# A graph layer on one core: the rank-five row term as four row-tiled passes instead of four full ones

## The chip, the cores and the metric

The kernel runs on one core of one Trainium2 chip. The metric is the device time of the launch in microseconds, as the median of several runs. A profile is one further execution, recorded instruction by instruction. The engines are called PE (TensorE, with its weight loads listed apart as PEld), DVE (VectorE), ACT (ScalarE), POOL (GpSimd) and SP (SyncE, which issues all DMAs here).

## The reference, cut to what matters

64 batch items, each with 256 tokens of 768 features and a 256 x 256 matrix `adj` of zeros and ones. With `h` the normalized, rectified input:

```python
h = jnp.maximum(_layernorm(x, axis=-1), 0.0)
ctx = jnp.matmul(adj, hs @ Wadj.T + badj) / deg_c[..., None]
ctx = ctx + jnp.matmul(radj, hs @ Wrev.T + brev) / rdeg_c[..., None]
ctx = ctx + hs @ Wself.T + bself
agg = jnp.einsum('bij,bijr->bir', adj, E[rels])
rel = agg @ Wr.T + br * deg[..., None]
...
rel = rel + ragg @ Wrr.T + brr * rdeg[..., None]
return ctx + rel
```

`deg` and `rdeg` are the row and column sums of `adj`; `rels` is `adj` itself. So the relation term of a token depends on its two degrees alone, and together with the biases it is, per token, a row of five numbers (two flags "degree over 0", a one, two degrees) times a 5 x 768 matrix. This small product is what the change is about.

## The kernel before, in words

**The large products.** The three products of `h` with the weights are made for both 128-token halves of an item by a scheme of 15 block products in place of 18 (`PRODUCTS`, line 24). Each operand is split into parts in the type fp32r. A block product (`product`, line 629) is 12 matmuls of 128x128 weights and 384 columns: eight in one part and four in the other (`first` and `second`, with the order of the two depending on the place in the chain), with a scaling of the sum in PSUM by ACT between them (line 657). DVE or ACT then read the sum into one or two blocks `c` (lines 668, 677, 679). The products are done in two sweeps over all items (`SWEEPS`, line 54): eight in the first, and in the second 9, 7, 6, 15, 12, 4 and 1, in this order. Products 9, 6, 12 and 1 share a chain `x`, which stays in one pair of PSUM banks; 7 has a pair called `v`, 15 one called `u`, and 4 one called `t`. Items 1 to 62 are "regular". Items 0 and 63 use plain fp32 matmuls instead (`whole`, line 754).

**Between the sweeps** the blocks lie in DRAM. In the second sweep `step2` (line 933) does the seven products of an item and the aggregations (`aggregate`, line 909): four groups of eight fp32r matmuls with `adj` as weights, each evicted by DVE at line 928 with the division by the degree.

**The row term before.** `front2` (line 838) writes the five numbers of each token into a 128x128 tile `cols`: for each half of the tokens, two copies, 32 columns apart. A transpose on PE (line 886) turns it over, and ACT copies 64 rows of the result into the tile `half0` and the other 64 into `half1` (line 892); the other 64 rows of each tile are zeros, written once at the start (line 1075). `rows_prepare` (line 789) makes the matching right side: the 5 x 768 matrix stands four times in 128 partitions, 32 apart, once as its high part and once as what is left, alternating. Then `add_rows` in `product` (line 645) adds `half.T @ rows` to the sum of product 7 (first half of the tokens) and of product 15 (second half), just before the second block is read from it, since only that one is to contain the row term. Each addition is two matmuls of 384 columns with a contraction over 128 partitions. Items 0 and 63 do the same into a fresh pair of banks (lines 939 to 954).

**The order of the work.** All operations are first recorded with an engine, a duration, a rank (a due time) and the buffers they use. `Plan.schedule` (line 303) then builds the order in which they are issued, by a simulation: each engine takes the ready operation of lowest rank for which buffers are free. The ranks are shifted by a table of numbers for each kind of operation, `OFFSETS` (line 91). Names in it end in `@` for item 0, `@1` for item 1, `$` for item 63, `$1` for item 62. PSUM is handed out as four pairs of banks (`"Q": 4` in `SLOTS`). Once issued, each engine runs its own operations strictly in order and waits for others by semaphores.

Of the kernel before, what the change touches and what calls it, by code (L numbers as in the profile page):

```python
# [10 lines left out]
F32 = mybir.dt.float32  # L11
# [6 lines left out]
P = 128  # L18
# [47 lines left out]
        (9, "x", 0, ((1, 0, 0),)),  # L66
        (7, "v", 0, ((1, 0, 2), (1, 0, 1))),
        (6, "x", 1, ((1, 0, 1),)),
# [23 lines left out]
    "a0+a1+b0+b1": 8.69, "a0+a1+b0+b1$1": -108.02, "a0+a1+b0+b1@1": -28.72, "a0+a2": 3.05, "a0+a2$1": 18.41,  # L92
    "a0+a2+b0+b2": -1.59, "a0+a2+b0+b2$1": -102.81, "a0+a2+b0+b2@1": -29.55, "a0+a2+b2": -16.06,
    "a0+a2+b2$1": -82.94, "a0+a2+b2@1": 11.49, "a0+a2@1": -97.83, "a1+a2": -2.38, "a1+a2$1": -81.56,
    "a1+a2@1": -53.12, "a1+b0+b1": 2.88, "a1+b0+b1$1": -81.79, "a1+b0+b1@1": -139.93, "a1+b1": 4.34,
    "a1+b1$1": -79.5, "a1+b1@1": -17.92, "a2+b2": -15.53, "a2+b2$1": 11.35, "a2+b2@1": -111.63, "adj": 10.35,
    "adj$": -18.98, "adj$1": 7.21, "adj@": -54.66, "adj@1": 0.9, "agg00": 21.54, "agg00$": -40.97, "agg00$1": 40.2,
    "agg00@": -20.22, "agg00@1": -77.59, "agg01": 12.58, "agg01$": -138.03, "agg01$1": -97.46, "agg01@": -128.81,
    "agg01@1": -13.92, "agg10": 14.41, "agg10$": -22.12, "agg10$1": 69.43, "agg10@": -6.37, "agg10@1": 14.14,
    "agg11": 15.02, "agg11$": 11.68, "agg11$1": 35.7, "agg11@": -41.86, "agg11@1": -9.17, "aggr": 3.18,  # L100
    "aggr$": 7.69, "aggr$1": -25.58, "aggr@": -100.4, "aggr@1": -52.75, "b0+b1": 3.69, "b0+b1$1": 5.96,
    "b0+b1@1": -45.99, "b1+b2": -1.41, "b1+b2$1": -76.7, "b1+b2@1": -148.88, "b2-a1": -12.05, "b2-a1$1": -9.74,
    "b2-a1@1": -11.89, "bias": -84.06, "c00": 3.83, "c00$1": -110.03, "c00@": -5.48, "c00@1": -3.61, "c01": 5.97,
    "c01$1": 20.35, "c01@": 6.13, "c01@1": 11.64, "c02": 12.75, "c02$1": 7.61, "c02@": -3.44, "c02@1": -9.92,
    "c10": 17.9, "c10$1": 92.49, "c10@": 12.31, "c10@1": -26.9, "c11": 16.65, "c11$1": 30.73, "c11@": -0.83,
    "c11@1": -8.71, "c12": -9.52, "c12$1": 18.61, "c12@": 10.68, "c12@1": 6.4, "centre0": -2.78, "centre0$": 14.67,
    "centre0$1": 12.9, "centre0@": 1.93, "centre0@1": -4.77, "centre1": -29.85, "centre1$": 16.76,
    "centre1$1": 3.95, "centre1@": 34.71, "centre1@1": -3.19, "cols": -92.86, "d": 3.75, "d$": -46.21, "d$1": 7.75,
    "d@": 40.53, "d@1": -44.55, "degree": 14.27, "degree$": -21.1, "degree$1": -31.5, "degree@": -2.83,
    "degree@1": -21.54, "diagonal": 16.77, "eT": -7, "eps": -1.93, "eps$": -108.36, "eps$1": -19.3, "eps@": 4.64,  # L110
    "eps@1": 4.47, "first 1": 10.98, "first 1$1": 25.72, "first 10": 12.02, "first 10$1": -4.97,
    "first 10@1": 14.89, "first 11": 5.53, "first 11$1": -75.81, "first 11@1": 7.68, "first 12": -30.38,
    "first 12$1": -130.69, "first 12@1": -16.6, "first 13": 8.05, "first 13$1": -88.9, "first 13@1": -145.94,
    "first 14": -19.82, "first 14$1": 25, "first 14@1": 17.03, "first 15": -16.89, "first 15$1": -109.2,
    "first 15@1": -49.67, "first 1@1": 21.05, "first 2": 9.57, "first 2$1": -4.16, "first 2@1": 23.27,
    "first 3": -11.06, "first 3$1": -20.24, "first 3@1": -128.99, "first 4": 13.54, "first 4$1": 36.84,
    "first 4@1": -2.43, "first 5": 3.35, "first 5$1": -15.95, "first 5@1": -319.17, "first 6": 12.54,
    "first 6$1": -59.61, "first 6@1": -48.93, "first 7": -21.55, "first 7$1": -130.17, "first 7@1": -46.94,
    "first 8": -6.63, "first 8$1": -130.81, "first 8@1": 14.25, "first 9": -18.3, "first 9$1": -16.06,
    "first 9@1": -56.83, "flag": 69.83, "h0": -1.22, "h0$1": 11.51, "h0@1": -9.15, "h1": 0.44, "h1$1": 6.56,  # L120
    "h1@1": -11.86, "half0": 6.84, "half0$": -10.24, "half0$1": -105.95, "half0@": -17.91, "half0@1": -53.11,
    "half1": -7, "half1$": -161.34, "half1$1": -112.57, "half1@": -4.5, "half1@1": -33.45, "high00": -17.72,
    "high00$": 7.67, "high00$1": 39.71, "high00@": -95.79, "high00@1": -132.39, "high02": 15.43, "high02$": -8.98,
    "high02$1": -27.43, "high02@": -10.87, "high02@1": 13.62, "high10": -1.41, "high10$": -5.84,
    "high10$1": 105.73, "high10@": -88.55, "high10@1": 19.43, "high12": 7.31, "high12$": 13.34, "high12$1": -29.03,
    "high12@": -55.9, "high12@1": -47.34, "keep c00": 7.41, "keep c00$1": 27.77, "keep c00@": -65.27,
    "keep c00@1": -79.13, "keep c01": 1.55, "keep c01$1": -12.24, "keep c01@": 38.39, "keep c01@1": -91.42,
    "keep c02": -17.39, "keep c02$1": 38.98, "keep c02@": 62.12, "keep c02@1": -58.71, "keep c10": -12.45,
    "keep c10$1": -185.49, "keep c10@": -48.48, "keep c10@1": -47.03, "keep c11@": -2.5, "keep c12": -22.45,
    "keep c12$1": 31.13, "keep c12@": -22.62, "keep c12@1": -25.9, "keep h0": -33.37, "keep h0$1": -2.51,  # L130
    "keep h0@1": -48.37, "keep h1": 16.04, "keep h1$1": -14.04, "keep h1@1": -19.88, "left0 1": 5.55,
    "left0 1$1": 15.94, "left0 10": 5.84, "left0 10$1": 4.52, "left0 10@1": -47.34, "left0 11": -32.11,
    "left0 11$1": -11.52, "left0 11@1": -104.63, "left0 12": 3.78, "left0 12$1": 33.37, "left0 12@1": -32.14,
    "left0 13": 3.38, "left0 13$1": 16.36, "left0 13@1": 9.79, "left0 14": 7.42, "left0 14$1": -64.24,
    "left0 14@1": 10.25, "left0 15": 6.36, "left0 15$1": 11.31, "left0 15@1": 10.98, "left0 1@1": -28.48,
    "left0 2": 9.1, "left0 2$1": -6.48, "left0 2@1": 9, "left0 3": -20.81, "left0 3$1": -158.45,
    "left0 3@1": -7.38, "left0 4": -7.17, "left0 4$1": 35.5, "left0 4@1": -1.66, "left0 5": -38.77,
    "left0 5$1": -42.67, "left0 5@1": -48.2, "left0 6": 2.23, "left0 6$1": 18.1, "left0 6@1": -2.29,
    "left0 7": -20.33, "left0 7$1": -43.73, "left0 7@1": -83.4, "left0 8": 2.58, "left0 8$1": -65.87,
    "left0 8@1": -23.62, "left0 9": -38.94, "left0 9$1": -103.7, "left0 9@1": -23.48, "left1 1": 13.87,  # L140
    "left1 1$1": -156.93, "left1 10": -33.63, "left1 10$1": -20.33, "left1 10@1": -75.44, "left1 11": 1.26,
    "left1 11$1": -21.37, "left1 11@1": -66.88, "left1 12": 0.51, "left1 12$1": 27.39, "left1 12@1": -125.37,
    "left1 13": 10.94, "left1 13$1": -237.77, "left1 13@1": 13.62, "left1 14": -7.94, "left1 14$1": -95.64,
    "left1 14@1": 17.17, "left1 15": -0.1, "left1 15$1": -0.79, "left1 15@1": -32.31, "left1 1@1": -26.63,
    "left1 2": -36.76, "left1 2$1": 8.05, "left1 2@1": -94.05, "left1 3": 2.6, "left1 3$1": 24.12,
    "left1 3@1": -171.62, "left1 4": 2.22, "left1 4$1": 6.46, "left1 4@1": -19.24, "left1 5": -20.28,
    "left1 5$1": -16.74, "left1 5@1": 10.07, "left1 6": -1.47, "left1 6$1": 16.61, "left1 6@1": -34.54,
    "left1 7": -12.59, "left1 7$1": 14.19, "left1 7@1": 7.51, "left1 8": 9.77, "left1 8$1": 15.63,
    "left1 8@1": 3.29, "left1 9": 3.68, "left1 9$1": -113.48, "left1 9@1": -52.25, "left2 1": -30.23,
    "left2 1$1": -170.63, "left2 10": -8.63, "left2 10$1": -27.62, "left2 10@1": 10.3, "left2 11": 5.94,  # L150
    "left2 11$1": 20.71, "left2 11@1": -162.72, "left2 12": -13.41, "left2 12$1": -131.98, "left2 12@1": -3.75,
    "left2 13": 8.66, "left2 13$1": 7.67, "left2 13@1": -6.15, "left2 14": -16.62, "left2 14$1": 10.35,
    "left2 14@1": 0.48, "left2 15": 8.03, "left2 15$1": 33.15, "left2 15@1": -19.54, "left2 1@1": -38.48,
# [254 lines left out]
def on_pe(n):  # L408
    return 0.00045 * n
# [6 lines left out]
def record(nc, plan, fixed, B, NREL, part=None):  # L416
# [201 lines left out]
    def passes(b, n, w, q, pairs, start, stop):  # L618
        r = words[n]
        for i, (lw, rw) in enumerate(pairs):  # L620
            for f in range(2):
                for half in range(2):
# [3 lines left out]
                        skip_group_check=not start,  # L626
                    )

    def product(b, s, spec, rank, banks, rows=None):
        n, chain, place, reads = spec  # L630
        w = split(b, n, s, rank)
        if chain not in banks:
# [621 lines left out]
```

## Time and profile before

| | us |
|---|---|
| median of three runs (2517.66 to 2519.09) | 2517.99 |
| profiled execution | 2519.23 |
| its span, first to last instruction | 2517.3 |
| first sweep of regular items, about | 20 to 1106 |
| row passes of regular items, first to last | 1198.5 to 2490.4 |

| in the second stretch | count | duration as shown, ns |
|---|---|---|
| row passes on PE into `v` (L647) | 124 | 337 |
| row passes on PE into `u` (L647) | 124 | 337 |
| row passes of items 0 and 63 (L944) | 8 | 340 |
| copies `half` on ACT (L892) | 128 | 272 |
| transposes on PE (L886) | 64 | 271 |
| reads of `v` on DVE (L677) | 124 | 953 |

The page gives for each engine the time in which at least one instruction was running. On PE consecutive matmuls overlap, so the 337 ns shown for one are longer than the distance to the next. The granted clock was 0.999 of full speed over the whole span.

### The profile page before, as it was taken

What the parts mean: (1) busy time and instruction counts of PE and PEld (TensorE: products, weight loads), DVE (VectorE), ACT (ScalarE), POOL (GpSimd) and SP (SyncE); (2) the same over time, 40 slices, a digit from 0 to 9 for tenths busy, and PEclk for the clock granted to TensorE, in tenths of its full rate; (3) what the DMA queues carried; (4) which work ended last, traced back from release to release, by engine and by line L of the source; (5) the groups of instructions that cost most, each with busy time, mean ns of one, the idle gap of its engine ahead of it and who ended that gap; (6) DMA issues with size and microseconds to landing.
All of it is one profiled execution on the core that took longest, in us unless ns stands there. A gap on an engine that the chain in (4) does not pass through costs nothing. (4 is left out here: it accounts for less than half of the span.)

```text
span 2517.3 us, 43767 instructions
## 1 busy us (share of the span) xinstructions
PE 2489.2 (99%) x13922; PEld 2412.2 (96%) x13922; DVE 2134.8 (85%) x3933; ACT 1814.3 (72%) x3901; POOL 1300.7 (52%) x1138
## 2 busy tenths in 40 slices
PE   7999999999999999999999999999999999999998
PEld 4899999999999999997999999999999999999998
DVE  7887778777777877778899999999999999999997
ACT  4788888888888888886666666666666666666664
POOL 1555555555555555542555555555555555555553
PEclk9999999999999999999999999999999999999999
DMA  5677777777777777785676666667666666766663
GB/s 209 244 275 282 265 267 285 272 264 274 279 268 269 283 274 270 278 295 189 190 226 213 210 210 207 209 212 213 212 209 206 213 210 211 212 211 211 216 212 130
DMA packets 223971, 590.64 MB, mean 235 GB/s; under 512 B 24036, under 2 KB 24292, under 8 KB 223736
## 3 DMA queue, kind: packets, MB, share of 16 engines
q1 hardware_dynamic: 223736, 587.79, 69.0%
q8 instruction: 112, 1.84, 0.3%
q14 instruction: 123, 1.01, 0.1%
HBM read 364.22 MB, written 223.48 MB: 233 GB/s over the span
## 5 line engine op out<-in xcount | busy, mean ns | idle before, releaser
L905 POOL TENSOR_TENSOR hl<-c,hl 128x768 fp32r<-128x768 f32 x256 | 490.5, 1936 | 400.1 <-ACT hl L901 347.5
L623 PE MATMUL y<-word,left 128*128 128x384 f32 x2976 | 573.2, 337 | 0.0
L623 PE MATMUL x<-word,left 128*128 128x384 f32 x2976 | 570.8, 336 | 1.5 <-ACT x L657 1.0
L623 PEld LDWEIGHTS y<-word,left 128*128 128x128 f32 x2976 | 521.3, 188 | 5.5 <-ACT y L657 0.4
L623 PEld LDWEIGHTS x<-word,left 128*128 128x128 f32 x2976 | 521.1, 188 | 4.5 <-ACT x L657 1.6
L917 PE MATMUL agg<-hl,a 128*128 128x384 f32 x2048 | 398.8, 338 | 0.1
L917 PEld LDWEIGHTS agg<-hl,a 128*128 128x128 f32 x2048 | 356.0, 188 | 15.0 <-DVE c L679 14.5
L728 POOL TENSOR_TENSOR h<-h,row 128x768 f32<-128x768 f32 x128 | 235.6, 1861 | 246.7 <-DMA row<-d 207.1
L901 ACT ACTIVATE hl<-c 128x768 fp32r<-128x768 f32 x256 | 203.2, 839 | 154.9 <-PE agg L917 142.6
L623 PE MATMUL w<-word,left 128*128 128x384 f32 x1488 | 304.1, 339 | 1.3 <-DVE x L776 1.3
L623 PE MATMUL z<-word,left 128*128 128x384 f32 x1488 | 301.2, 337 | 0.3 <-ACT left L595 0.2
L928 DVE SCALAR_TENSOR_TENSOR c<-agg,rd,c 128x768 f32<-128x768 f32 x252 | 252.8, 1003 | 28.7 <-PE agg L917 28.5
L657 ACT ACTIVATE x<-x 128x768 f32<-128x768 f32 x248 | 197.4, 796 | 96.6 <-PE x L623 95.0
L612 DVE SCALAR_TENSOR_TENSOR left<-left 128x256 fp32r<-128x256 f32 x434 | 266.0, 634 | 0.0
L623 PEld LDWEIGHTS z<-word,left 128*128 128x128 f32 x1488 | 260.2, 188 | 3.7 <-ACT left L595 0.5
L623 PEld LDWEIGHTS w<-word,left 128*128 128x128 f32 x1488 | 258.3, 188 | 4.4 <-DVE x L776 1.6
L657 ACT ACTIVATE y<-y 128x768 f32<-128x768 f32 x248 | 197.2, 795 | 43.4 <-PE y L623 40.2
L612 DVE SCALAR_TENSOR_TENSOR left<-left,top 128x256 fp32r<-128x256 f32 x496 | 199.8, 413 | 6.4
L677 DVE TENSOR_TENSOR c<-c,v 128x768 f32<-128x768 f32 x124 | 117.3, 946 | 81.2 <-PE v L647 79.5
L585 POOL TENSOR_TENSOR a1+a<-h 128x256 f32<-128x256 f32 x62 | 45.9, 740 | 271.1 <-DMA h<-kept_h 249.7
L602 ACT ACTIVATE top<-left 128x256 f32<-128x256 f32 x496 | 181.3, 383 | 6.0 <-DVE left L612 2.0
L706 POOL TENSOR_TENSOR cols<-cols,half 128x2 f32<-128x2 f32 x64 | 82.7, 1292 | 166.4 <-DVE cols L705 164.7
(137 smaller groups left out, 4441.4 us busy)
## 6 DMA issues: line engine op xcount, KB each, us to landing
c<-kept SPq DMA_DIRECT2D x316, 384.0 KB
kept<-c SPq DMA_DIRECT2D x252, 384.0 KB
x<-in_x_dram SPq DMA_DIRECT2D x128, 384.0 KB
h<-in_x_t_dram SPq DMA_DIRECT2D x128, 384.0 KB
out_dram<-c SPq DMA_DIRECT2D x126, 384.0 KB
kept_h<-h SPq DMA_DIRECT2D x124, 384.0 KB
h<-kept_h SPq DMA_DIRECT2D x124, 384.0 KB
adj<-in_adj_dram SPq DMA_DIRECT2D x64, 512.0 KB
```

The source lines that it names most:

```text
L585: lambda: nc.gpsimd.tensor_tensor(t(home), x[1](), y[1](), op=op),
L602: lambda: nc.scalar.activation(view(top), t(w)[:, 0].bitcast(F32), AF.Copy),
L612: lambda: nc.vector.scalar_tensor_tensor(t(w)[:, 2], t(w)[:, 1].bitcast(F32), -STEP, first(), op0=ALU.mult, op1=ALU.add), s == 1,
L623: nc.tensor.matmul(t(q)[:, half, : H // 2], t(w)[:, lw, f, :], t(r[rw])[:, f, ts(half, H // 2)], start=start and i == 0 and f == 0, stop=s ...
L657: lambda: nc.scalar.activation(view(), view(), AF.Copy, scale=scale),
L677: emit = lambda to=to, op=op: nc.vector.tensor_tensor(to(), to(), view(), op=op)
L706: pool(0.7, r - 21.5, f"pow {b}", [col], [col], lambda: nc.gpsimd.tensor_tensor(var(), var(), v["half"], op=ALU.pow))
L728: lambda h=h, one=one: nc.gpsimd.tensor_tensor(t(h), t(h), one(0), op=ALU.subtract),
L901: lambda: nc.scalar.activation(t(pair)[:, 0], t(o), AF.Copy, scale=LOWER),
L905: lambda: nc.gpsimd.tensor_tensor(t(pair)[:, 1], t(o), t(pair)[:, 0].bitcast(F32), op=ALU.subtract),
L917: nc.tensor.matmul(t(q)[:, half, : H // 2], t(s["a"])[:, c, k, ts(ic, P)], t(pairs[c])[:, part, ts(half, H // 2)], start=(c == 0 and part ...
L928: lambda q=q, to=to, ic=ic: nc.vector.scalar_tensor_tensor(to(), t(q)[:, :, : H // 2], t(rd)[:, ic, k : k + 1], to(), op0=ALU.mult, op1=AL ...
```

## The change

The row term gets a different layout, and its four passes of an item become four passes on row tiles of PE, issued together.

- `cols` holds each half's five numbers four times, 16 columns apart. After the transpose, each quarter of 32 partitions holds the numbers of one half of the tokens twice. One ACT copy brings the whole result into one tile, `token`. The `half` tiles with their zeros, and their memsets, are gone.
- `rows` holds the 5 x 768 matrix eight times, 16 partitions apart, the high part and the rest alternating. It is put together with a per-partition factor (`upper`, made from the identity by DVE), one more full-height ACT copy and one DVE operation, in place of two ACT copies of 32 partitions. The bias is loaded eight times instead of four.
- Each pass contracts over 32 partitions only. Four of them, each on its own row tile, write the two banks of product 7 and the two banks of product 15. They are issued as one operation, once both products are complete and the first block has been read from each; the second reads follow.
- In the second sweep product 6 stands ahead of 7, so that the order is 9, 6, 7, 15, 12, 4, 1.
- Items 0 and 63 use the same group of four passes.
- `OFFSETS`: 485 of 779 values are different, among them nearly all of the second sweep; 13 are added. Those of the first sweep differ only for items of the kinds `$`, `$1` and, in a few, `@1`.

```diff
     (
         (9, "x", 0, ((1, 0, 0),)),
+        (6, "x", 1, ((1, 0, 1),)),
         (7, "v", 0, ((1, 0, 2), (1, 0, 1))),
-        (6, "x", 1, ((1, 0, 1),)),
         (15, "u", 0, ((1, 1, 2), (1, 1, 1))),
...
+    def add_rows(b, rank, token, qs, start):
+        def run():
+            for g in range(4):
+                at = slice(32 * g, 32 * (g + 1))
+                nc.tensor.matmul(
+                    t(qs[g // 2])[:, g % 2, : H // 2], t(token)[at], t(v["rows"])[at, ts(g % 2, H // 2)],
+                    start=start, stop=True, skip_group_check=not start, tile_position=(32 * g, 0),
+                )
+
+        pe(0.55, rank, f"token rows {b}", [token, v["rows"], *qs], [*qs], run)
...
-        def add_rows():
-            for half in range(2):
-                nc.tensor.matmul(
-                    t(q)[:, half, : H // 2], t(rows), t(v["rows"])[:, ts(half, H // 2)],
-                    start=False, stop=True, skip_group_check=True,
-                )
...
-            if rows and i:
-                pe(2 * on_pe(H // 2) + 0.17, rank + 2.7, f"rows {n} {b}", [rows, v["rows"], q], [q], add_rows)
...
+        if s == 0 or n not in (7, 15):
+            for i in range(len(reads)):
+                read(i)
+            return
+        read(0)
+        return q, lambda: read(1)
...
         act(on_act(H), rank - 2.0, "rows", [brow], [hi], lambda: nc.scalar.activation(t(hi), t(brow), AF.Copy, scale=LOWER))
+        act(
+            on_act(H), rank - 1.5, "rows", [brow, upper], [rest],
+            lambda: nc.scalar.activation(t(rest), t(brow), AF.Copy, scale=t(upper)[:, :1]),
+        )
         dve(
-            on_dve(H), rank - 1.0, "rows", [brow, hi], [rows],
-            lambda: nc.vector.tensor_tensor(t(rows), t(brow), t(hi).bitcast(F32), op=ALU.subtract), True,
-        )
-        for q in (0, 2):
-            at = slice(q * 32, (q + 1) * 32)
-            act(
-                on_act(H), rank - 0.5, "rows", [hi], [rows],
-                lambda at=at: nc.scalar.activation(t(rows)[at], t(hi)[at].bitcast(F32), AF.Copy),
-            )
+            on_dve(H), rank - 1.0, "rows", [rest, hi, upper], [rows],
+            lambda: nc.vector.scalar_tensor_tensor(
+                t(rows), t(hi).bitcast(F32), t(upper)[:, 1:], t(rest), op0=ALU.mult, op1=ALU.add
+            ), True,
+        )
...
-        to = lambda k: t(col).rearrange("p (c k r) -> p c k r", c=C, k=2)[:, :, :, k : k + 2]
-        of = lambda: t(deg)[:, b].unsqueeze(2).to_broadcast([P, C, 2, 2])
+        to = lambda k: t(col).rearrange("p (c q r) -> p c q r", c=C, q=4)[:, :, :, k : k + 2]
+        of = lambda: t(deg)[:, b].unsqueeze(2).to_broadcast([P, C, 4, 2])
...
-        s["half"] = v["halves"][b % 2]
-        for c in range(C):
-            at = slice(c * 64, (c + 1) * 64)
-            act(
-                0.27, r - 0.5, f"half{c} {b}", [pt], [s["half"][c]],
-                lambda c=c, at=at: nc.scalar.activation(t(s["half"][c])[at], t(pt)[at, 0, :P], AF.Copy),
-            )
+        s["token"] = v["tokens"][b % 2]
+        act(
+            0.3, r - 0.5, f"token {b}", [pt], [s["token"]],
+            lambda: nc.scalar.activation(t(s["token"]), t(pt)[:, 0, :P], AF.Copy),
+        )
...
+        held = []
         for i, spec in enumerate(SWEEPS[1] if b in regular else ()):
-            product(b, 1, spec, r + 2.1 * i, banks, where.get(spec[0]))
+            more = product(b, 1, spec, r + 2.1 * i, banks)
+            if more:
+                held.append(more)
+            if len(held) == 2:
+                add_rows(b, r + 2.1 * i + 3.0, s["token"], [q for q, _ in held], False)
+                for _, read in held:
+                    read()
+                held = []
```

## The prediction

> **What bounds the kernel.** I read the page's busy table first, then the list of who waited for whom on PE, then busy time in the stretch that the change touches, then PE's timeline inside one batch item.
>
> ```profile
> PE 2489.2 (99%) x13922; PEld 2412.2 (96%) x13922; DVE 2134.8 (85%) x3933; ACT 1814.3 (72%) x3901; POOL 1300.7 (52%) x1138
> ...
> PE whole L765 <- DVE h L732: 10.3, 1, 10.3
> PE pt L709 <- POOL cols L706: 7.8, 1, 7.8
> PE w L623 <- DVE x L776: 1.3, 1, 1.3
> ...
> 1198.52:2490.18 1291.66, 1290.77 (x7346) 1270.36 (x7346) 1167.21 (x1942) 845.49 (x1948) 682.47 (x544) 1.00 0.68 209
> ```
>
> TensorE is busy 99% of the span; its two large waits stand once each in the first 20 us. The last line (columns: PE, PEld, DVE, ACT, POOL busy, granted clock, DMA share, GB/s) is the second sweep over the 62 regular items: PE idle for 0.9 us of 1291.7, at full clock, VectorE at 90%.
>
> A busy PE isn't yet a PE doing work, because its ends are modelled, so I check it by starts. The `v` row passes first start at 1198.52 and the last pair at 2490.18, 61 items later: 1291.66/61 = 21.17 us an item. An item issues 7 products of 12 passes, 32 aggregation passes and 4 row passes: 120 passes, and one transpose.
>
> ```profile
> 2005.49 1.55 PE L917 MATMUL agg<-hl,a 128*128 128x384 f32 x8
> 2006.88 0.51 PE L647 MATMUL u<-rows,half 128*128 128x384 f32 x2
> 2007.23 3.63 PE L623 MATMUL x<-word,left 128*128 128x384 f32 x20
> 2010.70 1.57 PE L623 MATMUL t<-word,left 128*128 128x384 f32 x8
> ...
> 2017.01 3.17 PE L917 MATMUL agg<-hl,a 128*128 128x384 f32 x16
> 2020.02 0.27 PE L886 MATMUL pt<-ident,cols 128*128 128x128 f32 x1
> 2020.04 0.94 PE L623 MATMUL v<-word,left 128*128 128x384 f32 x4
> 2020.82 0.88 PE L623 MATMUL x<-word,left 128*128 128x384 f32 x4
> ```
>
> The pace is the distance of starts, not the second column: twenty passes take 2010.70 - 2007.23 = 3.47 us, 0.1735 us each, and the two row passes 2007.23 - 2006.88 = 0.35, no less than other passes though most of their contraction rows are zeros. The transpose takes what is left between 2017.01 and 2020.82 after 20 passes: 3.81 - 3.47 = 0.34. Then 120 x 0.1735 + 0.34 = 21.16, the measured 21.17. So the stretch holds no hidden stall: whatever PE time the change saves or adds in an item should appear in the span, until another engine sets the period.
>
> **The part that counts: four passes become one group.** Removed per regular item: 2 + 2 row passes = 4 x 0.1735 = 0.69 us of PE. Added: four 32-partition passes of 384 columns, on four row tiles, into four different PSUM banks (two of `v`, two of `u`). No such group is in the trace, so its PE time, called X, is bounded.
>
> Lower end. If the four run side by side and nothing is lost around them, X is one pass. The Trainium skill ("TensorE: Matmul & The Clock Gate", Measured speedup vs the span model) says that tiles in different row groups start about 4 ns apart and take one matmul plus that; an estimate from it is 0.1735 + 3 x 0.004 = 0.19. The saving would be 0.50 us an item. No run here shows it.
>
> The rule against the change stands in "TensorEngine Tiling (Array Packing)", Key Properties: changing the tiling mode, as opposed to the tile, drains the TensorE. The group changes it twice per item, since full-size passes lie on either side. What a drain costs here: a pass is shown with 337 ns, against a pace of 0.1735, so 0.16 us of it normally lies under the next pass. And a weight load that couldn't be pulled ahead is seen after waits:
>
> ```profile
> 2498.60 1.55 PE L623 MATMUL t<-word,left 128*128 128x384 f32 x8
> ...
> 2503.80 1.66 PE L623 MATMUL x<-word,left 128*128 128x384 f32 x8 [0.77 <-ACT x L657]
> ```
>
> Eight passes in stream show 1.55, eight whose first load starts with them 1.66: 0.11 (other such places give 0.11 to 0.13; I use 0.12). By the rule in full, X = 0.1735 + 2 x (0.16 + 0.12) = 0.73, a loss of 0.04 an item, 2.5 us in all. By the nearest row, the transpose, also a pass of another kind between streams, the two borders cost less: its own streaming is a third of a [...] fp32 matmul of 384 columns (`whole` in the first stage starts its loads 0.64 apart: 20.60, 21.24, 21.88), 0.21, and 0.34 - 0.21 leaves 0.13 for entering and leaving together. That gives X = 0.30. It doesn't change the tiling, so I don't take it as it is.
>
> I choose between these: one pass and one open weight load at each border, X = 0.1735 + 2 x 0.12 = 0.41. The new planner cost in the diff (0.55, less the 0.17 that the planner takes as overlap) says 0.38, which I only note. Saved per item: 0.69 - 0.41 = **0.28 us**. 62 items: 17.4 us. Items 0 and 63 have four row passes each at the same pace, now one group: 2 x 0.28 = 0.6 us. Sum **18.0 us**.
>
> **What covers the rest.**
>
> - Joining the two products. `v` must now wait for `u`. In the item above the `v` rows go at 2001.66, the second part of `u` at 2003.40, its rows at 2006.88. A group at about 2006 keeps `v`'s pair of banks some 4 us longer and frees `u` no later. Of the 4 x 21.17 bank-pair-us in an item, v and u take about 10 each, t 6, the x chain some 18, four aggregations about 3 each: 56 of 85, then 60. Covered; without this cover an aggregation waits for the eviction before it (1.00 us), which PE would see.
> - What queues behind the group's wait. The group needs `token`, both products complete, and both first reads. PE is in order, so all later passes wait behind it if it is placed too early; the order puts it behind other products' passes, as now. The two delayed second reads (0.95 us each on DVE) feed only the output blocks, whose next users are aggregation evictions.
> - Moving product 6 ahead of 7 changes no number of passes, scales, splits or reads; the `x` chain's place numbers stay the same. Cost 0, bounded by ±0.1 us an item for a `scale` that comes late (the two largest such waits on `x` now: 1.0 us in all).
> - ACT: two `half` copies of 0.27 become one of about 0.3 us; 0.24 less per item on an engine that is 65% busy in this stretch: hidden, 0. DVE: same reads; `tok` writes are twice as wide, 128x8 at 0.16 us now; under 0.02 more: hidden.
> - Would DVE become the bound? 1167.2/61 = 19.1 us an item, against 21.17 - 0.28 = 20.9. Room of 1.8 us: no. POOL with 11.2 and ACT with 13.9 are further off.
> - Rows prepared: two tiny DVE operations, four bias transfers of 15 KB on SP's queue, one full ACT copy (0.84) in place of two quarter-height ones (0.84 each), all around 1150 us while PE runs `whole` passes. The chain from `pr` to `rows` loses one 0.84 step; after it the end item's row passes waited 0.2 us on it. 0, at most 0.3 either way.
> - Four DVE memsets of 0.165 us at 1.2 us go; the first statistics wait until 4.28 for x to land: 0.
> - The table of offsets. First-sweep values change only for the second and second-last items, so the first 1080 us stay as they are. All second-sweep values are new, so the order of that stretch is new. It can't gain much, as the present order is without a stall; I count 0. The last 37 us (PE busy 29.9) can move by 2 us either way.
>
> Against the profiled execution: 2519.2 us (span 2517.3 and 1.9 around it) - 18.0 = 2501.2. The median of the runs is 1.2 below the profiled one, so 2518.0 - 18.0 = **2500.0 us**.
>
> **Rivals.**
>
> *Full overlap:* X = 0.19 as above; 64 groups x 0.50 = 32 us: 2486. For it: four distinct bank targets and four distinct row groups. Against it: the border costs that the trace shows even for a transpose.
>
> *Loads one behind the other:* the four weight loads share one path, and only the streaming overlaps. X = 0.1735 + 4 x 0.12 = 0.65, saving 0.04 x 64 = 2.6 us: 2515.4, no measurable change (I call 0.2%, 5 us, what this kernel's runs can tell from none). For it: every full pass is paired with a load, and PEld is busy at PE's pace. Here the change doesn't do what it says, except for the streaming.
>
> *Switching eats it and more (slower):* place, the two borders of each group; the array drains at both (2 x 0.16), and the four tile loads and the following full load stand open (5 x 0.12): X = 0.1735 + 0.32 + 0.60 = 1.09, +0.40 x 64 = +26 us: 2544. It decides from X = 0.69 on. For it: the skill's drain rule, and that loads are open after every break in the trace. Against: the transpose's borders cost only 0.13 together.
>
> *A stall of the new order:* the joined group or a short bank makes PE wait more than 0.28 us an item; at 0.5 us, +0.22 x 62 = +14: 2532. Against it: PE has no such wait now, and DVE and PSUM have room.
>
> **How the numbers follow.** Chances: forecast 0.46 (its own range, X from 0.30 to 0.50, 2493 to 2506), full overlap 0.24, loads in a row 0.13, switching 0.11, stall 0.06. Faster by over 0.2%: 0.46 + 0.24 and a share of the third, 0.72. Within 0.2%: 0.12. Slower: the last two, nearly, 0.16. The range 2483 to 2522 holds the first three and the near part of the slower ones, and leaves out the rest of these and a gain beyond full overlap.
>
> **What would show it.** In the changed profile the group's four starts should lie within a few tens of ns to 0.1 us, and the distance from its first start to the next full pass is X: 0.3 to 0.5 if I am right, about 0.19 or 0.65 or above for the rivals. The item period should fall from 21.17 to 20.9 with PE's idle time in this stretch still under some us, and the half of the span before 1100 us should be unchanged. I am wrong if the tile starts are a pace of 0.17 apart, if PE's list of waits shows a wait for DVE or ACT at the group or at an aggregation about 62 times, or if the period falls by the same amount in no place but the tail.

## The result, and the profile after

| | before | after |
|---|---|---|
| median, us | 2517.82 (2517.61 to 2519.09) | 2496.08 (2495.06 to 2496.78) |
| ratio, 95% interval | | 0.9911 (0.9899 to 0.9924) |
| profiled execution; its span | 2519.23; 2517.3 | 2496.45; 2494.7 |
| row passes of regular items (before: into `v`), start of the first to that of the last item's | 1198.52 to 2490.18 | 1201.30 to 2473.21 |
| one item of this stretch (that over its 61 periods) | 21.17 | 20.85 |

The change makes the kernel 21.7 us faster; 2500.0 was forecast, inside the range. But the time did not come from where the forecast took it: nearly three quarters of it have nothing to do with row tiles. The same views of the changed kernel as before: the busy table, who waited on PE, and the stretch between the first and last row pass (PE, PEld, DVE, ACT, POOL busy).

```profile
PE 2467.6 (99%) x13922; PEld 2381.1 (95%) x13922; DVE 2091.7 (84%) x3939; ACT 1787.1 (72%) x3836; POOL 1285.3 (52%) x1138
...
PE whole L780 <- DVE h L747: 10.6, 1, 10.6
PE pt L724 <- POOL cols L721: 7.5, 1, 7.5
PE w L628 <- DVE x L791: 1.3, 1, 1.3
...
1201.30:2473.21 1271.91, 1271.67 (x7365) 1242.73 (x7364) 1127.70 (x1950) 821.00 (x1888) 662.72 (x543) 1.00 0.64 213
```

PE is still the bound, with the same two waits at the start and none in the stretch; DVE is at 89% there. PE's timeline around one group of row tiles:

```profile
2011.41 1.55 PE L942 MATMUL agg<-hl,a 128*128 128x384 f32 x8
2012.90 0.44 PE L638 MATMUL v<-rows,token 32*128 32x384 f32 x2
2012.90 0.44 PE L638 MATMUL u<-rows,token 32*128 32x384 f32 x2
2013.27 1.67 PE L628 MATMUL x<-word,left 128*128 128x384 f32 x8
2014.78 1.55 PE L942 MATMUL agg<-hl,a 128*128 128x384 f32 x8
```

All four tiles start within 10 ns. But from 2011.41 to 2014.78 PE does only 16 full passes and the group: 3.37 - 16 x 0.1735 leaves 0.59 us for the group, not the 0.41 of the forecast. Four full passes took 0.69, so a group saves about 0.1 us, 6 to 7 us in 62 items. What gave the rest stands in a view of *before* that the prediction had not read, the waits of PE's weight loads. Here is the line of before that matters:

```profile
PEld agg L917 <- DVE c L679: 14.5, 58, 0.4
```

In 58 of 62 items the weight loads of an aggregation waited for DVE. PE's own list shows nothing of it, because a matmul's shown end lies about 0.16 us after the next could start, and the wait hides under that. Before, at one such place:

```profile
2017.01 3.17 PE L917 MATMUL agg<-hl,a 128*128 128x384 f32 x16
...
2017.50 0.94 DVE L679 SCALAR_TENSOR_TENSOR c<-x,c 128x768 f32<-128x768 f32 x1
...
2018.49 1.36 PEld L917 LDWEIGHTS agg<-hl,a 128*128 128x128 f32 x8 [0.26 <-DVE c L679]
```

The second aggregation needs a free pair of PSUM banks; DVE frees one when it ends the last read of the `x` chain at 2018.44. Sixteen passes at the pace of 0.1735 are 2.78 us, but the next instruction started only at 2020.02, 3.01 us later: 0.23 us lost, without any row in PE's list of waits. DVE is what the loads wait for: at all 58 places they start 0.052 to 0.054 us after the end of this read. Summed over the 60 places in the stretch where two aggregations stand side by side, the sixteen passes take 12.9 us more than this pace gives. In the changed kernel the longest wait of weight loads in this stretch is another one:

```profile
PEld v L638 <- DVE c L685: 15.0, 60, 0.3
PEld x L628 <- issue: 11.0, 60, 0.2
```

Both belong to the group itself, entering and leaving it, as the loads of the place shown above say:

```profile
2012.89 0.18 PEld L638 LDWEIGHTS v<-rows,token 32*128 32x128 f32 x2 [0.25 <-DVE c L685]
...
2013.27 0.30 PEld L628 LDWEIGHTS x<-word,left 128*128 128x128 f32 x2 [0.18 <-issue]
```

Between full passes a load starts some 0.17 us ahead of its pass; at both borders it starts within 0.01 of it. The list names DVE for the entering, but the first tile comes 0.268 to 0.270 us after the last full pass in all 62 groups, also in the three where the read of `u` had ended 0.55 to 1.58 us before. So this is the price of the border and no wait for DVE. No aggregation waits for DVE any more.

### The profile page after: what moved, and what is told of

The parts are those of the page before. It is cut to its first block, busy times and chain, and to the rows that moved or that the text cites. A ratio compares the mean times of both kernels' runs of the same rounds, so it can differ in the third digit from the quotient of the medians.

```text
span 2494.7 us, 43472 instructions
## 1 busy us (share of the span) xinstructions
PE 2467.6 (99%) x13922; PEld 2381.1 (95%) x13922; DVE 2091.7 (84%) x3939; ACT 1787.1 (72%) x3836; POOL 1285.3 (52%) x1138
## 4 chain that ended last, share of the span: by engine, by line
PE 96%; DMA 1%; DVE 1%; ACT 1%; issue 0%; POOL 0%; SPq 0%; DVEq 0%; ACTq 0%; POOLq 0%
PE x L628 21%; PE y L628 20%; PE agg L942 14%; PE z L628 10%; PE w L628 10%; PE t L628 5%; PE v L628 5%; PE u L628 5%; PE whole L780 2%; PE v L638 1%; DMA raw<-in_Wadj_dram 0%; DMA raw<-in_Wself_dram 0%; PE right L502 0%; PE pt L724 0%; DVE right L555 0%
## 5 line engine op out<-in xcount | busy, mean ns | idle before, releaser
L930 POOL TENSOR_TENSOR hl<-c,hl 128x768 fp32r<-128x768 f32 x256 | 475.3, 1857 | 649.3 <-ACT hl L926 459.2
L628 PE MATMUL x<-word,left 128*128 128x384 f32 x2976 | 592.2, 340 | 0.2 <-DVE c L687 0.2
L666 ACT ACTIVATE x<-x 128x768 f32<-128x768 f32 x248 | 191.8, 794 | 140.1 <-PE x L628 139.9
L926 ACT ACTIVATE hl<-c 128x768 fp32r<-128x768 f32 x256 | 215.1, 841 | 32.1 <-DVE c L685 24.3
L617 DVE SCALAR_TENSOR_TENSOR left<-left 128x256 fp32r<-128x256 f32 x434 | 203.0, 489 | 0.1
L676 ACT ACTIVATE c<-y 128x768 f32<-128x768 f32 x124 | 100.9, 814 | 71.7 <-PE y L628 71.7
```

Source lines behind the costliest of these rows:

```text
L617: lambda: nc.vector.scalar_tensor_tensor(t(w)[:, 2], t(w)[:, 1].bitcast(F32), -STEP, first(), op0=ALU.mult, op1=ALU.add), s == 1,
L628: nc.tensor.matmul(t(q)[:, half, : H // 2], t(w)[:, lw, f, :], t(r[rw])[:, f, ts(half, H // 2)], start=start and i == 0 and f == 0, stop=s ...
L666: lambda: nc.scalar.activation(view(), view(), AF.Copy, scale=scale),
L676: lambda o=o, sign=sign: nc.scalar.activation(t(o).rearrange("p (k n) -> p k n", k=2), view(), AF.Copy, scale=sign * (1.0 if value_last el ...
L926: lambda: nc.scalar.activation(t(pair)[:, 0], t(o), AF.Copy, scale=LOWER),
L930: lambda: nc.gpsimd.tensor_tensor(t(pair)[:, 1], t(o), t(pair)[:, 0].bitcast(F32), op=ALU.subtract),
```

## The experiments

The question was how the 22 us divide between the tiles and the new order, and what a group costs. In the expectations theory A is the reading just given; theory B is the prediction's, in which the tiles give all.

**Full passes in the new order.** The changed kernel, the same operations in the same order, but the four passes of an item over all 128 rows:

```diff
-                    t(qs[g // 2])[:, g % 2, : H // 2], t(token)[at], t(v["rows"])[at, ts(g % 2, H // 2)],
-                    start=start, stop=True, skip_group_check=not start, tile_position=(32 * g, 0),
+                    t(qs[g // 2])[:, g % 2, : H // 2], t(token)[:, g // 2], t(v["rows"])[:, ts(g % 2, H // 2)],
+                    start=start, stop=True, skip_group_check=not start,
...
```

(Not shown: `token` gets one block for each half of the tokens, with zeros outside of 32 rows, filled by two copies instead of one.)

> The changed kernel with its order of work kept operation for operation, but the four passes of an item again over the full 128 rows (token numbers of one half in 32 rows, zeros in the other 96), no row tiles. Two theories of the 22 us. Theory A (what the two traces suggest): a group of row tiles costs 0.59 us of PE and not 0.41, so the tiles save only 0.70 - 0.59 = 0.11 us an item, 7 us in all, and the rest comes from the new order, which has lost a wait of about 0.23 us an item at the aggregations: this kernel takes about 2503 us. Theory B (the prediction's): the order gives nothing, the tiles all of it: about 2518 us.

> The changed kernel once more, beside the two above: 2496 again, so that the tiles' share (against the 2502.3 of the full passes in the same order) rests on a second measurement; the difference should be 6 us, 4 to 8.

> The full passes in the changed kernel's order once more, same chip as the changed kernel: theory A 6 to 7 us above it, theory B 18 or more above it.

| measured side by side | median, us | ratio to before, 95% interval |
|---|---|---|
| before | 2518.73 | |
| full passes, new order | 2502.23 | 0.9932 (0.9919 to 0.9946) |
| the changed kernel again | 2495.82 | 0.9907 (0.9892 to 0.9922) |

A first measurement of the full passes gave 2502.29 beside 2519.07 for the kernel before. So the change without its tiles, which is mainly the new order, takes away 16.5 us, and the tiles 6.4 on top. That is theory A. The timeline of the full passes, the same place in the order as shown above:

```profile
2014.36 1.55 PE L945 MATMUL agg<-hl,a 128*128 128x384 f32 x8
2015.75 0.51 PE L637 MATMUL v<-rows,token 128*128 128x384 f32 x2
2016.10 0.51 PE L637 MATMUL u<-rows,token 128*128 128x384 f32 x2
2016.46 1.55 PE L628 MATMUL x<-word,left 128*128 128x384 f32 x8
2017.84 1.55 PE L945 MATMUL agg<-hl,a 128*128 128x384 f32 x8
```

3.48 us for 20 full passes, against 3.37 with the group: 0.11 us an item. No aggregation waits for DVE in this kernel's list. Its stretch (1199.69 to 2478.59) is 12.8 us shorter than that of before, 0.21 an item, and the lost time of the side-by-side aggregations was 12.9: in the stretch the vanished wait accounts for the whole gain of the order. The other 5.2 us of the 18.0 by which its span is shorter lie ahead of and behind the stretch, 1.8 of them in the last 100 matmuls of the run (26.1 us to the end before, 24.3 here); which waits they are stays open.

**One set of tiles more, three tiles less.** The edit is the loop of the group. For the regular items the row term is added twice, or three quarters of it are left out:

```diff
-            for g in range(4):
+            for g in range(4) if start else (0, 1, 2, 3) * 2:
...
-            for g in range(4):
+            for g in range(4 if start else 1):
```

> The changed kernel with the group issued twice in a row for the regular items (the row term is added twice), same order. Theory A with tiles side by side and the borders paid once: a second set of four tiles costs one pass, 0.17 us, +11 us: about 2507. If a tile's second weight load has to wait for its own first pass (0.12 more): +18 us, 2514. If loads of tiles follow one another: 4 x 0.05 to 0.1 more, 2520 or above. If each set pays everything again: 0.59, 2533.

> The changed kernel with one tile pass of the group of four in the regular items (three quarters of their row term are left out), same order. Theory A, tiles side by side with a fixed border of 0.41 us: one tile costs what four cost, within 0.02 us an item: 2495 to 2497. If the four weight loads follow one another (0.05 to 0.1 each): 9 to 18 us less, 2478 to 2487.

Twice: 2506.19 us (2505.50 to 2507.28), 10 us more. One tile: 2494.20 (2494.07 to 2494.47), 1.6 us less than four. The timeline of the doubled group, then that of the single tile:

```profile
2017.37 1.55 PE L942 MATMUL agg<-hl,a 128*128 128x384 f32 x8
2018.85 0.44 PE L638 MATMUL v<-rows,token 32*128 32x384 f32 x2
2018.86 0.44 PE L638 MATMUL u<-rows,token 32*128 32x384 f32 x2
2019.13 0.34 PE L638 MATMUL v<-rows,token 32*128 32x384 f32 x2
2019.14 0.34 PE L638 MATMUL u<-rows,token 32*128 32x384 f32 x2
2019.40 1.66 PE L628 MATMUL x<-word,left 128*128 128x384 f32 x8
2020.90 1.37 PE L942 MATMUL agg<-hl,a 128*128 128x384 f32 x7
```

```profile
2009.30 1.55 PE L942 MATMUL agg<-hl,a 128*128 128x384 f32 x8
2010.78 0.44 PE L638 MATMUL v<-rows,token 32*128 32x384 f32 x1
2011.15 1.67 PE L628 MATMUL x<-word,left 128*128 128x384 f32 x8
2012.66 1.55 PE L942 MATMUL agg<-hl,a 128*128 128x384 f32 x8
```

From aggregation to aggregation: 3.36 us with one tile, 3.37 with four, 3.53 with eight. The item's period rises by 0.17 us with the second set (21.02 against 20.85), and with one tile it is 20.85 as with four, so most of the 1.6 us lie outside of the stretch. So four tiles do run side by side, in the time of one full pass, their loads too, and the group's 0.59 us is 0.17 of work and about 0.42 of borders. The borders can be read off: the first tile starts 0.10 late after the eight passes before it (2011.41 + 8 x 0.1735 = 2012.80, against 2012.90), the next full pass starts 0.37 after the tiles and not 0.17, and its eight passes take 0.12 longer, as after other waits in these traces. Whether it is the array running empty or only the loads that can't be taken ahead, these runs do not separate.

**Two groups of two tiles in the old order.** The kernel before, in its order, with each product's two row passes as two tiles:

```diff
+                g = 2 * (n == 15) + half
+                at = slice(32 * g, 32 * (g + 1))
...
-                    t(q)[:, half, : H // 2], t(rows), t(v["rows"])[:, ts(half, H // 2)],
-                    start=False, stop=True, skip_group_check=True,
+                    t(q)[:, half, : H // 2], t(rows)[at], t(v["rows"])[at, ts(half, H // 2)],
+                    start=False, stop=True, skip_group_check=True, tile_position=(32 * g, 0),
...
```

(Not shown: `cols` and `rows` get the layout with 16 rows that the changed kernel has, and the row passes of items 0 and 63 become tiles too.)

> The kernel before with its order kept operation for operation, but the two row passes of each product on two row tiles of 32 rows, so two groups of two tiles an item instead of four full passes. Theory A: nearly all of a group's 0.59 us is fixed, so two groups cost 1.18 in place of 0.70, +0.48 us an item, +30 us: about 2547 us, and the wait at the aggregations is still in the trace. Theory B, a group at 0.41: +0.12 an item, +7 us: about 2525. If tiles save in proportion and borders cost nothing (0.19 a group): 0.38 in place of 0.70, 2498.

2542.51 us (2542.39 to 2542.92), ratio 1.0094 (1.0078 to 1.0109): 23.4 us slower, where 30 were expected. The borders are paid twice an item, and row tiles without the join lose. The lines below are from PE's timeline and from the waits of its loads.

```profile
2018.53 0.44 PE L649 MATMUL v<-rows,half 32*128 32x384 f32 x2
2018.90 1.68 PE L923 MATMUL agg<-hl,a 128*128 128x384 f32 x8
...
PEld agg L923 <- issue: 11.2, 60, 0.2
```

Two tiles take as long to the next pass, 0.37, as four did. In the list two aggregations wait for DVE where 58 did: against expectation that wait is gone, most likely since the longer groups ahead give DVE time to free the bank. It had cost some 13 us; the expected 30 less 13 is 17, and from the first to the last row pass the two traces differ by 18 (1299.9 and 1317.8 us). The other 5 lie outside of this stretch and were not followed up.

**The group left out.** The regular items lack the row term.

```diff
-            for g in range(4):
+            for g in range(4 if start else 0):
```

> The changed kernel with the group of row passes left out for the 62 regular items (their outputs lack the row term), same order. What the group costs is read as the difference. Theory A, 0.59 us a group: 2496 - 36.6 = about 2459.5 us. Theory B, 0.41: about 2471. Full overlap without borders, 0.19: 2484. A difference smaller than the trace's 0.59 with waits for DVE would mean that another engine is next.

2479.50 us (2477.75 to 2479.94), 16.6 below the changed kernel and not 36.6, so this number alone would have fitted a group of 0.27 us. The waits of PE's loads and two engines' timelines say why it isn't one:

```profile
PEld agg L942 <- PE x L628: 21.7, 59, 0.6
...
2002.92 0.95 DVE L685 TENSOR_TENSOR c<-c,u 128x768 f32<-128x768 f32 x1
...
2003.98 1.36 PEld L942 LDWEIGHTS agg<-hl,a 128*128 128x128 f32 x8 [0.36 <-PE x L628]
```

The aggregation behind the group now waits 0.36 us. The list names PE; but DVE ended the second read of `u` at 2003.87, and in 59 of 60 such places the loads start 0.115 to 0.116 us after the end of this read, while their distance from PE's last pass varies from 0.33 to 0.63. Taking work away here uncovers the next wait for a bank pair. With the group in place the same read ended at 2014.35, and the loads of the aggregation, at 2014.61, did not wait. PE could come forward by only 0.27 us an item (16.6 over 62) before the wait took the rest: by this estimate the join has some 0.3 us of cover, no more.

**The hidden wait alone.** The kernel before, with one exchange in PE's order after it has been built:

```diff
+            if names[0][:3] == "agg" and names[0][:4] == names[1][:4] and names[2:] == ["turn2", "second 7"]:
+                at = todo.index(b)
...
+                    todo.remove(d)
+                    todo.insert(at, d)
```

> The kernel before, unchanged but for one exchange in PE's order: in each regular item the four passes that complete product 7 go between the two aggregations that stood next to each other, instead of behind them. Theory A: the second of these aggregations waited about 0.23 us for its pair of PSUM banks, which DVE's last read of the x chain frees, and the exchange gives DVE 0.69 us more: -13 us, about 2506, and the wait is gone from PE's loads. Theory B: what looked like a wait was the price of the transpose that follows (0.34 us as the prediction took it), which stays: no change, 2519. If the delay only moves on (the eviction and the next bank come 0.69 later): between these or slower.

2539.93 us (2538.00 to 2540.87), 21 us slower. Where theory A aimed it was right: the aggregation no longer waits. But see PE and then its loads a little later:

```profile
2033.10 1.55 PE L917 MATMUL agg<-hl,a 128*128 128x384 f32 x8
2034.49 0.27 PE L886 MATMUL pt<-ident,cols 128*128 128x128 f32 x1
2034.52 0.94 PE L623 MATMUL x<-word,left 128*128 128x384 f32 x4
2035.76 1.66 PE L623 MATMUL u<-word,left 128*128 128x384 f32 x8 [0.30 <-DVE c L928]
...
PEld u L623 <- DVE c L928: 36.0, 58, 0.6
```

Product 15 needs the bank pair that this aggregation held, and gets it 0.69 later, after the eviction by DVE at line 928: at 58 places its loads start 0.053 or 0.054 us behind the end of it. The wait has moved from the aggregation to `u` and grown to 0.62 as the loads show it. The exchange also settles what the transpose costs: from 2033.10 to 2034.49 the eight passes take 1.39 with no residue, so the 0.34 that the prediction gave to the transpose was 0.23 of waiting and 0.1 of transpose.

## Why the prediction came out right, point by point

The total held by luck: two errors of opposite sign nearly cancelled. 18.0 us were forecast for the tiles and 0 for the order, against 6.4 and 16.5.

- **"So the stretch holds no hidden stall": wrong.** The sum of the starts was right, but its residue of 0.34 was given to the one unexplained instruction, the transpose, without a look at what the weight loads waited for. With 0.23 of it a wait, "it can't gain much ... I count 0" for the new order fell too: without the tiles the change is worth 16.5 us.
- **X, the PE time of a group: mis-sized.** 0.41 was taken, 0.59 measured. The part inside was as the lower end had it: tiles side by side, 0.17. The borders were taken as two open loads, 0.24, and are 0.42. The drain rule that speaks against the change, in full 0.56, was nearer than the row of the transpose (0.13), which was itself misread (the last point below) and doesn't change the tiling. Entering is no dearer than an open load (0.10); what was missed is that leaving holds the next full pass back by 0.20 before its load stands open for 0.12.
- **Loads one behind the other:** refuted, since a group of one tile and a group of four differ by 0.01 us from aggregation to aggregation.
- **Switching eats it and more (slower):** not for the joined group, 0.59 being below the deciding 0.69; it is what happens to the pairs, where the same borders serve two passes instead of four.
- **Joining the products is covered:** held, PE waits for nothing at the group. The margin is thinner than the count of bank-pairs suggested, as the kernel without the group shows: free pairs on the average don't help when the next pair is freed by one late DVE read.
- **A stall of the new order:** not there. The opposite, a stall of the old order, was not among the rivals.
- **DVE not the bound, ACT hidden, memsets and row preparation nothing:** held. ACT is busy 27 us less in all and nothing of it is seen; DVE is busy for 18.5 us an item of the 20.85. The last transpose of the first sweep (`pt` at line 724, before at line 709) starts at 1107.59 against 1105.98, and at 1105.76 in the kernel with full passes: unchanged within 2 us, as forecast.
- **The signs named in advance** would have passed a wrong account: the period fell to 20.85, next to the forecast 20.9, and the distance from the group's first start to the next full pass is 0.37, inside the "0.3 to 0.5" named as right. But this distance leaves out the 0.10 ahead and the 0.12 behind, and the period doesn't tell tiles from order. X has to be measured from a full pass before to a full pass after.
- **The transpose's row: misread.** Its streaming was taken as a third of 0.64 us. But only the first `whole` matmuls, from 18.5 to 22.5 us, start 0.64 apart; after that it is half as much, and also just ahead of the transpose at 1155.98:

```profile
1153.40 2.74 PE L765 MATMUL whole<-raw,h 128*128 128x384 f32 x8
...
1155.98 0.27 PE L886 MATMUL pt<-ident,cols 128*128 128x128 f32 x1
```

2.58 us for eight are 0.3225 each, and a third of that is 0.11, not 0.21. Then 0.34 - 0.11 = 0.23 would have been left over, which is just the wait of the example. The profile gives the clock as 1.00 in both places, so why the first ones are slower stays open.

## What to carry to other kernels

Row tiles that run side by side take the time of one pass, but going from full passes to tiles and back costs about 0.42 us here. So join them until four passes share one pair of borders, since two lose (three were not run; by the same sum they would take 0.59 in place of 0.52). When PE is shown 99% busy, count its passes by their starts and then read what its *weight loads* waited for; a stall shorter than the overlap of two matmuls, here 0.16 us, stands only there. And when an edit brings a new order along, measure the order with the old operations first: it can be the larger part, and a wait for a PSUM bank that is moved by hand may come back larger at the next user of the bank.

## What the runs showed of the hardware

Four 32-row tiles start within some 10 ns of one another, and a second set of four follows 0.28 us after the first and ends up costing 0.17 us of the item, the price of a single full pass. The first tile comes 0.10 us late whether a product or an aggregation stands before it, and with two tiles as with four (262 to 270 ns from the start of the last full pass to that of the first tile, over all groups of both kernels). A transpose in fp32 between fp32r passes costs about 0.1 us of PE, though it is shown with 0.27. A weight load that is held by a DVE read starts 0.053 us after the read's end; in the kernel without the group, where a semaphore instruction stands between the two, 0.115.
